# Value and output projections in visits of two token tiles, PSUM places for side work only within a step of its due time

## The chip, the cores and the metric

The kernel runs on one core of one Trainium2 chip. The metric is the device time of one execution in microseconds (us); lower is better. The core has five engines with an instruction queue each: TensorE (PE in the profile, its weight loads PEld), VectorE (DVE), ScalarE (ACT), GpSimd (POOL) and SyncE (SP, which here only issues DMAs). Each engine works through its own queue in order, and engines wait for each other through semaphores.

## What is computed

A block of a diffusion transformer with adaptive layer norm, on x of 2 x 2048 x 256 in fp32: attention with 16 heads, then a gated feed-forward network with 704 hidden units whose inputs and weights are rounded to a 4-bit float in blocks of 16.

```python
h = _layernorm(x, axis=-1) * (1 + ca) + sa
q = einsum('bnd,hkd->bnhk', h, query_proj)      # 16 heads, key size 16
k = einsum('bnd,hkd->bnhk', h, key_proj)
v = einsum('bnd,hvd->bnhv', h, value_proj)      # value size 64
sim = einsum('bnkh,bmhk->bnhm', q, k)
attn = softmax(sim * 0.25, axis=1)              # over the queries n
o = einsum('bnhm,bmhv->bnhv', attn, v)
x = x + ga * einsum('bnhv,dhv->bnd', o, output_proj)
h = _layernorm(x, axis=-1) * (1 + cb) + sb
h = silu(fp4_linear(h, w_gate)) * fp4_linear(h, w_up)
x = x + gb * fp4_linear(h, w_down)
```

The softmax runs over the queries, so one tile of 128 keys m with all 2048 queries is complete in itself.

## The kernel before

**Steps.** The attention is 512 steps: 2 batch entries x 16 heads x 16 tiles of 128 keys. A step computes the scores of one key tile against all 2048 queries in two halves of 1024 (tile `ps`). VectorE takes each half out of PSUM into `e`, scaled and negated, with its minimum. GpSimd combines the two minima (`mn`), ScalarE does the exponential of all 2048 with its sum (`z`), VectorE the reciprocal `rz`, GpSimd scales the 64 values of the key tile by it (`vn`), and TensorE multiplies `vn` with `e` and adds to the head's output `o` (function `step`). `scores` writes the halves.

**Side work.** Everything else is threaded between the steps: projections of q and k (`qk`), of values for four heads at a time (`values`, "quad" q, tile `v`), the output projection of four heads, added to x (`project`, tile `op`), the rounding and transposing of the feed-forward weights, the layer norm of the second batch entry, and the whole feed-forward network of the first. Only the feed-forward network of the second batch entry comes behind the attention, as a tail (`tail`).

**Three uses of the TensorE array.** The scores contract over 64 rows (a stacked q and k), so two matmuls lie side by side in the rows of the array (profile form `64*128`). `o`, `v`, `op` and most of `qk` and the network of the first batch entry write 64 output rows each, two side by side in the columns (`128*64`; function `twin`). Transposes and the tail use the full array (`128*128`). The planner calls these modes "rows", "columns" and "full".

**PSUM.** Two banks hold `o` (pool `ps_o`). The other six are three places of two banks, room `s` (1024 fp32 per partition each). A half of scores takes a whole place. Side work takes a place and also the one token of room `misc` (`OTHER = ["s", "misc"]`), so that at most one side job holds a place at a time; `leave` gives both back.

**The planner.** Each job is a generator that hands out operations (`Op`) and waits (`Wait`). The class `Order` merges them, with estimated durations, into one order for each of TensorE, VectorE, ScalarE and GpSimd when the program is built; the chip sees only that order. A job gets a due time in steps (`add`), becomes active `AHEAD = 5` steps before it, and `settle` lets it pass a `Wait` when its keys are done and its rooms have something free. Among operations that could start within a patience of the earliest, the one with the earliest due goes first (`run`). `order.step` follows the last score group that was emitted.

**Groups of scores.** Two halves at least are emitted together, as one `Group`. When TensorE gets to it, `run` calls `grow`, which adds a third half (limit `GROUP = 3`) if a place is free by then. A group is one visit to the "rows" mode.

**Values and output projection.** `values(b, q, g)` does four token tiles (g runs over four groups of them): 16 matmuls into the whole place, then one copy of 128 x 1024 into `v` by ScalarE or VectorE, whichever the planner finds sooner (`copy`). `project(b, q, g)` likewise does four token tiles, and VectorE adds the 128 x 1024 to x. There are 32 such value visits and 28 such projection visits; the last quad's output projection of the second batch entry is another function, `project_last`. `spread_over` spreads the due times of a quad's visits over a stretch of steps: for values from 13 steps ahead of the quad to 3 into it.

Of the kernel before, what the change touches and what calls it, by code (L numbers as in the profile page):

```python
# [10 lines left out]
F32 = mybir.dt.float32  # L11
# [4 lines left out]
ALU = mybir.AluOpType  # L16
# [4 lines left out]
P = 128  # L21
EPS = 1e-5

MISC = 1
AHEAD = 5
PPE = 0.12
CHANGE = 0.1
PDVE = 0.04
PACT = 0.05
GROUP = 3  # L30
LAG = 4.5
HALF = 0.22
WPACE = 0.5
# [75 lines left out]
class Order:  # L109
# [7 lines left out]
    def __init__(self, rooms, ahead, patience):  # L117
        self.rooms = {name: [(0.0, i) for i in range(n)] for name, n in rooms.items()}
        self.ahead, self.patience = ahead, patience
        self.clock = dict.fromkeys(self.SAME, 0.0)  # L120
        self.done, self.counts = {}, {}
        self.later, self.active = [], []
        self.step, self.seq, self.table, self.chain = 0.0, count(), None, None
        self.port = 0.0
        self.mode = None

    def add(self, gen, due, pace=0.0):

# [27 lines left out]
    def settle(self, c):  # L156

        while isinstance(c.what, Wait):
            w = c.what
            if any(k not in self.done for k in w.after):  # L160
                return False
            if any(len(self.rooms[r]) < w.take.count(r) for r in w.take):
                return False
            times = [self.done[k] for k in w.after]
            taken = [heapq.heappop(self.rooms[r]) for r in w.take]
            times += [t - (w.early if n else 0.0) for n, (t, _) in enumerate(taken)]
            c.base = max([c.base] + [t + self.CROSS for t in times])
            self.advance(c, [place for _, place in taken])
            if c not in self.active:
                return False  # L170
        return True

    def run(self):
        while self.later or self.active:
# [6 lines left out]
            for c in sorted(self.active, key=lambda c: c.due):  # L181
# [25 lines left out]
                for f in found:  # L207
                    best.setdefault(f[4][0].engine, []).append(f)
            if not best:
                if not self.later:  # L210
                    raise RuntimeError(
                        "no chain can go on: "
                        + str([(c.due, vars(c.what)) for c in self.active[:20]])
                    )
                self.step = self.later[0][0] - self.ahead
                continue
            picks = []
            for e, found in best.items():
# [5 lines left out]
                picks.append((start, due, next(self.seq), c, ops))  # L224
            start, _, _, c, ops = min(picks)
            e = ops[0].engine
            t = start
# [98 lines left out]
def adaln_block(  # L326
# [585 lines left out]
    def qk(b, blk, i, n):  # L912

        room = "v" if (b, blk) == (0, 0) and (i == 1 or n % 2) else "st"
        place, _, _ = yield Wait([("ht", b, n), "wk" if i else "wq"], [*OTHER, room])
        if (b, i, blk) not in scratch:
            scratch[b, i, blk] = dram.tile(
                [P, 2, N], F32, tag=f"qk{i}_{blk}", name=f"scr{b}_{i}_{blk}"
            )
        ps = banks(place, f"qk{b}_{blk}_{i}_{n}")[:, 0, :]  # L920
        cols = slice(n * 512, (n + 1) * 512)
        pairs = [
            (wqk_sb[:, i, k, blk * P : (blk + 1) * P], h_t[b][:, k, cols]) for k in range(KC)
        ]
        if (b, blk) == (0, 0):
            for op in matmuls(ps, pairs):
                yield Free(op)
        else:
            ops = twin(ps, pairs)
            for k in range(KC):  # L930
                yield Free(ops[2 * k : 2 * k + 2])
        name = f"st{b}_{blk}_{i}_{n}"
        if room == "v":
            st = vp.tile([P, 4, QV], F32, tag="v", name=name).bitcast(F32R)
            st = st.rearrange("p (r u) n -> p r (u n)", r=2)
        else:
            st = w2.tile([P, 2, 512], F32R, tag="st", name=name, bufs=1)
        yield A.copy(st[:, 0, :], ps)
        yield V.tensor_tensor(st[:, 1, :], ps, st[:, 0, :], ALU.subtract)
        leave(place)  # L940
        st = st.bitcast(F32)
        if (b, blk) == (0, 0):
            if (0, 0) not in heads:
                yield Wait(take=["head"])
                new_head(0, 0)
            q, k = heads[0, 0]
            if i == 0:
                c = n // 2
                yield from stack_q(q, st[0:KD], n % 2, slice(c * 512, (c + 1) * 512))
                signal("first q", of=NCH)  # L950
            else:
                yield from stack_k(k, st[0:KD], cols)
                signal(("first k", n))
        c = n if i == 1 else q_chunk(n)
        yield S.dma_start(scratch[b, i, blk][:, :, c * 512 : (c + 1) * 512], st)
        give(room)
        signal(("qk", b, blk), of=2 * NCH)
        if b == 0 and blk == NB - 1:
            signal("h free", of=2 * NCH + NG)

    def load_head(b, h):
        yield Wait([("qk", b, h // HB)], ["head"])
# [19 lines left out]
        )  # L982
        signal(("wv", b, q))

    def values(b, q, g):
        yield Wait([("ht", b, g), ("wv", b, q)], ["v"])
        v = vs[b, q, g] = vp.tile([P, 4, QV], F32, tag="v", name=f"v{b}_{q}_{g}")
        place, _ = yield Wait(take=OTHER)
        ps = banks(place, f"v{b}_{q}_{g}")
        for j in range(4):  # L990
            m = 4 * g + j
            yield Free(
                twin(
                    ps[:, j // 2, j % 2 * QV : (j % 2 + 1) * QV],
                    [
                        (h_t[b][:, k, m * P : (m + 1) * P], wvs[b, q][:, k, :])
                        for k in range(KC)
                    ],
                )
            )  # L1000
        yield copy(
            v.rearrange("p (i j) n -> p i j n", i=2),
            ps.rearrange("p i (j n) -> p i j n", n=QV),
        )
        leave(place)
        signal(("v", b, q, g))
        if signal(("v", b, q), of=NG):
            give("wv")
        if b == 0 and q == NQUAD - 1:
            signal("h free", of=2 * NCH + NG)  # L1010


    o_acc = {}
# [4 lines left out]
    def scores(i, b, h):  # L1018
# [3 lines left out]
        while n < 2 * NT:  # L1022
# [27 lines left out]
            def grow(t):  # L1050
# [5 lines left out]
                    return False  # L1056
                if n % 2 == 0 and not (order.rooms["e"] and order.rooms["e"][0][0] <= t):
                    return False
                if order.rooms["s"][0][0] > t:
                    return False  # L1060
                half(heapq.heappop(order.rooms["s"])[1])
                return True

            for place in places:
# [9 lines left out]
    def step(i, b, h, m):  # L1074
# [21 lines left out]
        yield A.activation(e, e, AF.Exp, bias=mn[:, 2:3], scale=-1.0, accum_out=z)  # L1096
        rz = small.tile([P, 1], F32, tag="rz", name=f"rz{b}_{h}_{m}")
        yield V.reciprocal(rz, z)
        yield Wait([("v", b, h // 4, m // 4)])
        vn = small.tile([P, VD], F32, tag="vn", name=f"vn{b}_{h}_{m}")  # L1100
        yield G.tensor_scalar(
            vn,
# [58 lines left out]
                G.tensor_tensor(w[:, j, :], w[:, j, :], mod(b, "ga"), ALU.mult)  # L1161
        signal(("wo", b, q))

    def project(b, q, g):

        last = [("out", b, q - 1, 4 * g + j) for j in range(4)] if q else []
        place, _ = yield Wait([("osb", b, q), ("wo", b, q), ("x", b, g)] + last, OTHER)
        ps = banks(place, f"op{b}_{q}_{g}")
        for j in range(4):
            t = 4 * g + j  # L1170
            yield Free(
                twin(
                    ps[:, j // 2, j % 2 * D : (j % 2 + 1) * D],
                    [
                        (o_sb[b, 2 * q + k][:, t * P : (t + 1) * P], wos[b, q][:, k, :])
                        for k in range(2)
                    ],
                )
            )
        if signal(("projected", b, q), of=NG):  # L1180
# [10 lines left out]
        for j in range(4):  # L1191
            signal(("out", b, q, 4 * g + j))

    def project_last(b, q, t, n):

# [307 lines left out]
        add(qk(0, 0, 1, g), -48 if g == 0 else 4 * g - 3.5)  # L1503
    add(load_wv(0, 0), -40)
    for g in range(NG):
        add(values(0, 0, g), -5 if g == 0 else 4 * g - 3)
# [21 lines left out]
    for b in range(B):  # L1528
# [6 lines left out]
        for q in range(NQUAD):  # L1535
            e0 = s0 + 4 * q * NT
            if (b, q) != (0, 0):
                add(load_wv(b, q), e0 - 2 * NT)
                spread_over([values(b, q, g) for g in range(NG)], e0 - NT + 3, e0 + 3)
            add(load_wo(b, q), e0 + 2 * NT)  # L1540
            if (b, q) == (B - 1, NQUAD - 1):
                continue
            o0 = e0 + 4 * NT + 2
            spread_over(
                [project(b, q, g) for g in range(NG)], o0, o0 + (20 if q == NQUAD - 1 else 40)
            )
        if b < B - 1:
            f0 = s0 + PER + 10
# [68 lines left out]
```

## Time and profile before

| what | value |
|---|---|
| median of three runs | 1956.62 us (1956.03 to 1957.0) |
| profiled execution, its own time | 1956.12 us |
| its span, first to last instruction | 1953.7 us |
| TensorE matmul busy | 1910.6 us, 98% |
| VectorE busy | 1704.3 us, 87% |
| ScalarE busy | 1327.6 us, 68% |
| GpSimd busy | 619.8 us, 32% |
| DMA | 88.00 MB, mean 45 GB/s |
| mean granted TensorE clock | 0.999 |

Busy is the time in which at least one instruction of the engine was under way. Matmuls overlap each other, so a group's mean duration times its count is more than its busy time; what counts for TensorE is the distance from the start of one stretch of matmuls to the start of the next. In the timeline, an entry "x8" means eight records merged. A plain fp32 matmul leaves two records, the scores' matmul (a rounded fp32 type) one, so "ps ... x4" is two halves of scores and "o ... x8" the output matmuls of one step. The profile knows nearly all operations under one line, L264, since a helper records them; they are told apart by their tiles.

### The profile page before, as it was taken

Reading aid. Unit: us, or ns where it says so; the run is one execution under the profiler, and the core shown is the slowest. Engines: PE = TensorE matmul, PEld = TensorE weight load, DVE = VectorE, ACT = ScalarE, POOL = GpSimd, SP = SyncE. Lnnn points to the kernel's source line nnn. Section 1 sums busy time; section 2 is a strip of 40 time slices with the busy share of each in tenths; the row PEclk is TensorE's granted clock in tenths of the full one; section 3 lists DMA queues with packets and bytes.
Section 4 is the critical chain, followed back from the end, with each engine's and each line's share of the span. In section 5 each row is a group of like instructions: output and inputs, shape, how many; then the busy total and the mean of one; then the engine's idle time right before and its main releaser. Section 6 shows DMA issues by size and latency. Waiting matters only on the chain. (4 is left out here: it accounts for less than half of the span.)

```text
span 1953.7 us, 30223 instructions
## 1 busy us (share of the span) xinstructions
PE 1910.6 (98%) x10212; PEld 782.6 (40%) x10212; DVE 1704.3 (87%) x4114; ACT 1327.6 (68%) x1427; POOL 619.8 (32%) x1387
## 2 busy tenths in 40 slices
PE   8999999999999999999999999999999999999998
PEld 5323333333333333343334444334433333335666
DVE  5899989999999998889898788888788878997997
ACT  3677767777777677776777567667677877784333
POOL 0233333333334331112444344454353211230010
PEclk9999999999999999999999999999999999999999
DMA  6321121112111122121012201211011111100000
GB/s 205 82 64 53 46 60 49 39 34 50 33 46 33 39 66 81 55 71 46 18 47 60 52 27 45 55 36 26 21 36 44 33 33 33 39 1 1 12 17 17
DMA packets 40393, 88.00 MB, mean 45 GB/s; under 512 B 6320, under 2 KB 22576, under 8 KB 36272
## 3 DMA queue, kind: packets, MB, share of 16 engines
q1 hardware_dynamic: 38880, 83.98, 16.8%
q10 hardware_dynamic: 1360, 2.10, 0.3%
q8 instruction: 82, 1.34, 0.3%
q14 instruction: 71, 0.58, 0.1%
HBM read 63.51 MB, written 20.97 MB: 43 GB/s over the span
## 5 line engine op out<-in xcount | busy, mean ns | idle before, releaser
L264 DVE TENSOR_SCALAR_CACHE_REDUCE e<-ps 128x1024 f32<-128x1024 f32 x1024 | 1225.4, 1216 | 123.9 <-PE ps L264 96.1
L264 ACT ACTIVATE e<-e,mn 128x2048 f32<-128x2048 f32 x512 | 1025.2, 2003 | 417.6 <-POOL mn L264 412.5
L264 PE MATMUL o<-e,vn 128*64 128x512 f32 x4096 | 991.8, 603 | 14.6 <-POOL vn L264 10.4
L264 PEld LDWEIGHTS o<-e,vn 128*64 128x64 f32 x4096 | 252.9, 136 | 479.8 <-issue 380.0
L264 POOL TENSOR_SCALAR mn<-mn 128x1 f32<-128x1 f32 x512 | 153.7, 300 | 751.6 <-DVE rz L264 287.8
L264 PE MATMUL ps<-q,k 64*128 64x512 f32 x2048 | 379.7, 447 | 5.5 <-DVE e L264 2.0
L264 PEld LDWEIGHTS ps<-q,k 64*128 64x128 f32 x2048 | 157.9, 184 | 367.1 <-DVE rz L264 92.0
L264 POOL TENSOR_SCALAR vn<-v,rz 128x64 f32<-128x64 f32 x512 | 167.2, 327 | 348.6 <-DVE rz L264 263.0
L264 PE MATMUL op<-wo,osb 128*64 128x256 f32 (+1 forms) x960 | 122.9, 382 | 3.1 <-DVE x L264 1.8
L264 PE MATMUL v<-wv,ht 128*64 128x256 f32 x1024 | 122.1, 385 | 0.6 <-DVE st L264 0.6
L264 DVE RECIPROCAL rz<-z 128x1 f32<-128x1 f32 x512 | 80.4, 157 | 24.5 <-ACT e L264 23.8
L264 PEld LDWEIGHTS op<-wo,osb 128*64 128x64 f32 (+1 forms) x960 | 73.9, 140 | 57.2 <-issue 18.9
L264 ACT ACTIVATION_READ_ACCUMULATOR e<-e,mn 128x1 f32 x512 | 95.5, 186 | 0.0
L264 PEld LDWEIGHTS v<-wv,ht 128*64 128x64 f32 x1024 | 71.2, 138 | 53.8 <-issue 16.3
L264 DVE DVE_READ_ACCUMULATOR e<-ps 128x1 f32 x1024 | 84.8, 83 | 0.0
L264 ACT COPY osb<-o 64x512 f32<-64x512 f32 x106 | 61.3, 579 | 7.4 <-PE o L264 5.9
L264 PE MATMUL qk<-ht,wqk_sb 128*64 128x512 f32 (+1 forms) x224 | 62.6, 598 | 1.7 <-ACT ht L264 0.9
L264 POOL TENSOR_TENSOR h<-h,m 128x704 f32<-128x704 f32 x32 | 54.2, 1692 | 11.6 <-DVE m L264 3.2
L264 DVE TENSOR_TENSOR x<-op,x 128x1024 f32<-128x1024 f32 (+2 forms) x33 | 37.0, 1122 | 15.6 <-PE op L264 15.3
L264 PE MATMUL dn<-wdb,e 117*128 117x256 f32 (+1 forms) x192 | 45.0, 382 | 3.3 <-ACT e L264 3.1
L264 PE MATMUL dn<-wd_t,h2t 117*64 117x256 f32 (+1 forms) x384 | 46.8, 381 | 0.0
L264 ACT ACT_TABLE_LOAD x34 | 43.6, 1283 | 4.3 <-issue 3.7
(242 smaller groups left out, 1449.8 us busy)
## 6 DMA issues: line engine op xcount, KB each, us to landing
k<-scr SPq DMA_DIRECT2D x124, 256.0 KB, 4.8
scr<-st SPq DMA_DIRECT2D x32, 512.0 KB, 3.1
q<-scr SPq DMA_DIRECT2D x124, 128.0 KB, 5.8
x<-in_x_dram SPq DMA_DIRECT2D x8, 512.0 KB, 4.6
wv<-in_wv_dram SPq DMA_DIRECT2D x8, 256.0 KB, 3.0
wo<-in_wo_dram SPq DMA_DIRECT2D x8, 256.0 KB, 4.0
xt<-in_x_dram SPq DMA_DIRECT2D x4, 512.0 KB, 7.5
out_dram<-h2t SPq DMA_DIRECT2D x16, 128.0 KB, 1.7
```

The lines of the kernel that those rows point to most:

```text
L264: op = Op(self.name, *self.estimate(method, args, kw, lambda: f(*args, **kw)))
```

## The change

`values` and `project` take a parameter `half` and do two token tiles into one bank of the place, with a copy or add of 128 x 512; a quad has eight visits of each in place of four, spread over the same stretch of steps. A value tile `v` is allocated by its first half. A wait in `step` for the values is for the half that holds its key tile.

`settle` holds back a job that wants the `misc` token while it is due more than `PLACE_AHEAD = 1.0` steps ahead of the current step, unless no job at all can go on (`force`).

`grow` takes a place for the third half also when it comes free up to `PATIENCE = 0.1` us later than TensorE would get there; the planner adds that wait to the cost of the first matmul of this half.

```diff
+PLACE_AHEAD = 1.0
+PATIENCE = 0.1
@@ settle
             if any(len(self.rooms[r]) < w.take.count(r) for r in w.take):
                 return False
+            if "misc" in w.take and c.due > self.step + PLACE_AHEAD and not self.force:
+                return False
@@ run
             if not best:
+                if not self.force:
+                    self.force = True
+                    continue
...
+            self.force = False
@@ values
-    def values(b, q, g):
-        yield Wait([("ht", b, g), ("wv", b, q)], ["v"])
-        v = vs[b, q, g] = vp.tile([P, 4, QV], F32, tag="v", name=f"v{b}_{q}_{g}")
+    def values(b, q, g, half):
+        after = [("ht", b, g), ("wv", b, q)]
+        if half == 0:
+            yield Wait(after, ["v"])
+            vs[b, q, g] = vp.tile([P, 4, QV], F32, tag="v", name=f"v{b}_{q}_{g}")
+            signal(("v room", b, q, g))
+        else:
+            yield Wait([*after, ("v room", b, q, g)])
+        v = vs[b, q, g]
         place, _ = yield Wait(take=OTHER)
-        ps = banks(place, f"v{b}_{q}_{g}")
-        for j in range(4):
-            m = 4 * g + j
+        ps = banks(place, f"v{b}_{q}_{g}_{half}")[:, 0, :]
+        for j in range(2):
+            m = 4 * g + 2 * half + j
...
-        yield copy(
-            v.rearrange("p (i j) n -> p i j n", i=2),
-            ps.rearrange("p i (j n) -> p i j n", n=QV),
-        )
+        yield copy(v[:, 2 * half : 2 * half + 2, :], ps.rearrange("p (j n) -> p j n", n=QV))
         leave(place)
@@ grow
-                if order.rooms["s"][0][0] > t:
+                free, place = order.rooms["s"][0]
+                if free > t + PATIENCE:
                     return False
-                half(heapq.heappop(order.rooms["s"])[1])
+                heapq.heappop(order.rooms["s"])
+                first = len(group)
+                half(place)
+                group[first].cost += max(0.0, free - t)
                 return True
@@ step
-        yield Wait([("v", b, h // 4, m // 4)])
+        yield Wait([("v", b, h // 4, m // 4, m % 4 // 2)])
@@ project
-    def project(b, q, g):
+    def project(b, q, g, half):
...
-        for j in range(4):
-            t = 4 * g + j
+        for j in range(2):
...
-        x4 = xs[b, g]
-        yield V.tensor_tensor(
-            x4.rearrange("p (i j) d -> p i j d", i=2),
-            ps.rearrange("p i (j d) -> p i j d", d=D),
-            x4.rearrange("p (i j) d -> p i j d", i=2),
-            ALU.add,
-        )
+        x2 = xs[b, g][:, 2 * half : 2 * half + 2, :]
+        yield V.tensor_tensor(x2, ps.rearrange("p (j d) -> p j d", d=D), x2, ALU.add)
@@ where the jobs are added
-                spread_over([values(b, q, g) for g in range(NG)], e0 - NT + 3, e0 + 3)
+                spread_over(
+                    [values(b, q, g, half) for g in range(NG) for half in range(2)],
+                    e0 - NT + 3,
+                    e0 + 3,
+                )
```

More of the change, by code (lines that the diff above doesn't have):

```diff
@@ L224, in run @@
                 picks.append((start, due, next(self.seq), c, ops))
+            self.force = False
             start, _, _, c, ops = min(picks)
@@ L958, in qk @@
         if b == 0 and blk == NB - 1:
-            signal("h free", of=2 * NCH + NG)
+            signal("h free", of=2 * NCH + 2 * NG)
     def load_head(b, h):
@@ L983, in load_wv @@
         signal(("wv", b, q))
[L985 to L987 removed]
+    def values(b, q, g, half):
[7 more added lines that the diff above has]
+        v = vs[b, q, g]
         place, _ = yield Wait(take=OTHER)
[L989 to L991 removed]
+        ps = banks(place, f"v{b}_{q}_{g}_{half}")[:, 0, :]
+        for j in range(2):
+            m = 4 * g + 2 * half + j
             yield Free(
                 twin(
[L994 removed]
+                    ps[:, j * QV : (j + 1) * QV],
                     [
@@ L1000, in values @@
             )
-        yield copy(
-            v.rearrange("p (i j) n -> p i j n", i=2),
-            ps.rearrange("p i (j n) -> p i j n", n=QV),
-        )
+        yield copy(v[:, 2 * half : 2 * half + 2, :], ps.rearrange("p (j n) -> p j n", n=QV))
         leave(place)
-        signal(("v", b, q, g))
-        if signal(("v", b, q), of=NG):
+        signal(("v", b, q, g, half))
+        if signal(("v", b, q), of=2 * NG):
             give("wv")
         if b == 0 and q == NQUAD - 1:
-            signal("h free", of=2 * NCH + NG)
+            signal("h free", of=2 * NCH + 2 * NG)
     o_acc = {}
@@ L1162, in load_wo @@
         signal(("wo", b, q))
-    def project(b, q, g):
-        last = [("out", b, q - 1, 4 * g + j) for j in range(4)] if q else []
+    def project(b, q, g, half):
+        t = 4 * g + 2 * half
+        last = [("out", b, q - 1, t + j) for j in range(2)] if q else []
         place, _ = yield Wait([("osb", b, q), ("wo", b, q), ("x", b, g)] + last, OTHER)
-        ps = banks(place, f"op{b}_{q}_{g}")
-        for j in range(4):
-            t = 4 * g + j
+        ps = banks(place, f"op{b}_{q}_{t}")[:, 0, :]
+        for j in range(2):
             yield Free(
                 twin(
-                    ps[:, j // 2, j % 2 * D : (j % 2 + 1) * D],
+                    ps[:, j * D : (j + 1) * D],
                     [
-                        (o_sb[b, 2 * q + k][:, t * P : (t + 1) * P], wos[b, q][:, k, :])
+                        (o_sb[b, 2 * q + k][:, (t + j) * P : (t + j + 1) * P], wos[b, q][:, k, :])
                         for k in range(2)
@@ L1179, in project @@
             )
-        if signal(("projected", b, q), of=NG):
+        if signal(("projected", b, q), of=2 * NG):
             give("osb", 2)
             give("wo")
-        x4 = xs[b, g]
-        yield V.tensor_tensor(
-            x4.rearrange("p (i j) d -> p i j d", i=2),
-            ps.rearrange("p i (j d) -> p i j d", d=D),
-            x4.rearrange("p (i j) d -> p i j d", i=2),
-            ALU.add,
-        )
+        x2 = xs[b, g][:, 2 * half : 2 * half + 2, :]
+        yield V.tensor_tensor(x2, ps.rearrange("p (j d) -> p j d", d=D), x2, ALU.add)
         leave(place)
-        for j in range(4):
-            signal(("out", b, q, 4 * g + j))
+        for j in range(2):
+            signal(("out", b, q, t + j))
     def project_last(b, q, t, n):
@@ L1505, in adaln_block @@
     for g in range(NG):
-        add(values(0, 0, g), -5 if g == 0 else 4 * g - 3)
+        for half in range(2):
+            add(values(0, 0, g, half), -5 if g == 0 else 4 * g - 3)
     steps = [(b, h, m) for b in range(B) for h in range(H) for m in range(NT)]
@@ L1544, in adaln_block @@
             spread_over(
-                [project(b, q, g) for g in range(NG)], o0, o0 + (20 if q == NQUAD - 1 else 40)
+                [project(b, q, g, half) for g in range(NG) for half in range(2)], o0, o0 + (20 if q == NQUAD - 1 else 40)
             )
```

## The prediction

> **What bounds the kernel now.** I read the shares of busy time first, then the same by stage, then TensorE's waits, then TensorE's timeline.
>
> ```profile
> PE 1910.6 (98%) x10212; PEld 782.6 (40%) x10212; DVE 1704.3 (87%) x4114; ACT 1327.6 (68%) x1427; POOL 619.8 (32%) x1387
> ```
>
> ```profile
> 105.00:800.00 695.00, 679.60 (x3572) 242.34 (x3570) 648.58 (x1543) 509.39 (x526) 239.74 (x588) 1.00 0.19 48
> 800.00:1780.00 980.00, 973.83 (x5470) 376.88 (x5467) 824.36 (x1874) 707.76 (x737) 351.17 (x743) 1.00 0.15 38
> 1780.00:1954.00 174.00, 158.67 (x675) 115.38 (x674) 154.94 (x472) 56.69 (x96) 13.66 (x11) 1.00 0.04 13
> ```
>
> The second view gives, for each stretch, its length and then the busy time of PE, PEld, DVE, ACT and POOL. TensorE is busy for all but 15 us of 695 and all but 6 of 980: it is the bound of the attention. VectorE is close behind it in the first 800 us (93%) and well behind later (84%). So only what TensorE does or waits for moves the end, and in the first 800 us more work on VectorE could become a wait.
>
> ```profile
> PE o L264 <- POOL vn L264: 10.4, 17, 1.8
> ...
> PE o L264 <- ACT osb L264: 2.5, 3, 1.6
> PE ps L264 <- DVE e L264: 2.0, 5, 0.7
> ```
>
> These are TensorE's waits: total, times, longest. Inside the attention it mostly waits for the scaled values `vn`, the last link of the chain that begins with the scores. Waits for a place that VectorE has to empty (`ps` on `e`) are 2.0 us in the whole run.
>
> ```profile
> 423.54 0.73 PE L264 MATMUL ps<-q,k 64*128 64x512 f32 x4
> 424.21 1.94 PE L264 MATMUL o<-e,vn 128*64 128x512 f32 x8
> 426.07 0.73 PE L264 MATMUL ps<-q,k 64*128 64x512 f32 x4
> 426.74 2.79 PE L264 MATMUL o<-e,vn 128*64 128x512 f32 x12
> 429.36 1.03 PE L264 MATMUL v<-wv,ht 128*64 128x256 f32 x8
> 430.33 0.73 PE L264 MATMUL ps<-q,k 64*128 64x512 f32 x4
> ...
> 436.26 0.97 PE L264 MATMUL ps<-q,k 64*128 64x512 f32 x6
> 437.16 2.79 PE L264 MATMUL o<-e,vn 128*64 128x512 f32 x12
> 439.89 0.73 PE L264 MATMUL ps<-q,k 64*128 64x512 f32 x4
> ```
>
> TensorE's timeline, start and duration. Starts are what to read. A visit to the scores with two halves lasts 426.74 - 426.07 = 0.67 us, one with three 437.16 - 436.26 = 0.90: a half costs 0.23, and 0.67 - 0.46 = 0.20 is the fixed price of the visit. The `o` stretch of 12 records that is followed by `v` (same mode) lasts 429.36 - 426.74 = 2.62 us, the one followed by scores 439.89 - 437.16 = 2.73: leaving the column mode costs 0.11. Without a change of mode eight records are 0.86 to 0.87 (values, half the columns); the `v` stretch between `o` and scores is 0.97 (leaving: +0.10), and another between scores and `o`, from 420.81 to 421.73, is 0.92 (entering: +0.05). So one visit to the scores costs 0.20 + 0.10 + 0.05 = 0.35 us beside its work.
>
> [...] here VectorE alone empties the scores, 1024 times 1216 ns, and is at 93% early. [...] a copy of 1024 out of PSUM takes 1222 ns and one of 512 takes 683 ns, so the split costs 2 x 683 - 1222 = 144 ns.
>
> **The change, part by part.** A planner writes the order, so I counted in the listings of both programs' instructions, engine by engine.
>
> *TensorE, work.* Both have the same 6348 matmuls with the same shapes; halving a visit changes no matmul. Changes of mode fall from 1094 to 1032. Visits to the scores fall from 504 to 471: those with two halves from 456 to 343, those with three from 32 to 107. 33 visits less at 0.35 us are 11.5 us; changes between the column and the full mode rise from 86 to 90, at about 0.1 us each (fitted over the stretches) 0.4 us. Fitted over all 1389 stretches of the trace (a price per matmul by shape, one per kind of change) and summed over each program's listing, TensorE's own work goes from 1893.5 to 1882.7 us. I take **-10.9 us**, in full on the path since TensorE is the bound. The fit leaves 60 us of the span as waits: 43.1 seen as idle, 16.9 inside stretches that begin late.
>
> *The wait in a group.* There are 75 more visits of three halves, and the third may be planned to wait up to 0.1 us for VectorE to hand over its place. Bounds 0 and 75 x 0.1 = 7.5 us; no row of before shows it. Behind it on TensorE's queue are the `o` matmuls, but they would have started only after the same visit. I take the middle, **+3.7**.
>
> *Waits for `vn`.* From a step's first score matmul to its first `o` matmul there lie on average 10.67 us of TensorE work before and 11.87 after, by the listings and the prices above. Steps with less than 7 us are 54 before and 19 after; less than 6 us, 18 and 4. The chain between them is two evictions, minimum, exponential with its sum, reciprocal and scaling: 2 x 1.15 + 0.30 + 2.0 + 0.19 + 0.16 + 0.33 = 5.3 us and the hand-overs. The short ones are those that waited. Bounds: 10.4 us gone, or none. I take half gone, **-5**.
>
> *VectorE.* Value copies there are 10 of 1024 before, 28 of 512 after (ScalarE: 22 of 1024, then 36 of 512); adds to x are 28 of 1024, then 56 of 512. Start to start by the trace's durations, VectorE's work over the whole program goes from 1674 to 1685 us, +11. In the first 224 steps it goes from 661 to 666 while TensorE's goes from 687.5 to 682.6: the margin shrinks from 26 to 17 us, and waits for places should grow. Bounds: none, since TensorE's side is still the larger, or the whole 11 us. I take **+2.5**, a little over a second time the 2.0 us of `ps` on `e`.
>
> *The places.* 64 + 56 visits in place of 32 + 28 hold a place, each from its first matmul to the next user's for 4.1 us (values) and 4.9 us (projections) of TensorE work on average, before 8.0 and 10.4; the sum is 576 before, 554 after. That is why more scores come in threes. The restriction to one step ahead moves side work later. The last value visit of a quad starts 7 to 10 us ahead of its first `o`, before 8 to 15; a copy of 512 takes 0.6, so nothing is late.
>
> *Queues.* Values and projections issue no DMA, but the loads of `wv` and `wo` wait for their ends: on SP's queue they move behind the k and q loads of one head; the values' own loads are asked for 32 steps ahead. The q and k projections' writes move too; the last for the second batch entry is 49 us of TensorE work ahead of its first scores (before 34), and a write and a load land in 3.1 and 4.8 us. On POOL the `wo` scaling moves with its load, 34 steps ahead of the first projection. All free. The last 424 matmuls, the tail, are the same in the same order.
>
> Sum: -10.9 + 3.7 - 5 + 2.5 = **-9.7 us**. The profiled execution took 1956.1 us (span 1953.7 and 2.4 around it), 0.5 below the median of the runs; from the median I get 1956.6 - 9.7 = **1946.9 us**.
>
> **Rivals.** *More of it:* scores run so far ahead that nearly all `vn` waits and part of the hidden 16.9 us go, and the places in threes are free in time: -10.9 - 10 + 2 = -19, 1938 us. For it: the short distances fall to a third. Against: of the 43 us of idle time 3.9 lie ahead of the first scores and 15.3 behind the last step, where the order stays.
>
> *Eaten up:* VectorE's extra 11 us all come onto the path early on: -10.9 + 11 = 0, 1956.6 us. For it: 93% busy in that stage. Against: TensorE's sum stays the larger there.
>
> *Slower:* the short side visits hand their place over quickly. A place left by a side job is taken again with less than 1.8 us of TensorE work between in 103 of 300 cases, before in 57 of 240. A copy of 0.6 us that comes behind a score eviction of 1.15 with hand-overs needs some 2.0 to 2.3, so TensorE could wait 0.5 us at each of the 46 new ones: +23 - 10.9 = +12, 1969 us. It decides when 30 of the 46 wait that long. For it: both engines are nearly full. Against: of the 57 before, almost none shows as a wait (`ps` on `e` 5 times).
>
> *Not what it says:* the listing shows the halved visits and longer groups, so this falls away.
>
> **How the numbers follow.** Forecast 0.63 (1942 to 1952), more of it 0.17, eaten up 0.11, slower 0.09. What a measurement tells from no change here is 0.2%, 3.9 us. Faster is the first two and a little of the third's edge: 0.82; same 0.09; slower 0.09. The range that leaves out two in ten, over the bounds of the unknown terms (-10.9 + 7.5 on one side, nearly -19 on the other): 1939 to 1953.
>
> **What would show it.** Right: `ps` stretches of x6 become about a quarter of the score visits, and the starts still give 0.35 us for a visit; `o` on `vn` falls below 10.4 us; TensorE's busy time falls by about 10 with its share still 98%; the tail lasts as long as before. Wrong: `ps` on `e`, or `op` and `v` on their copies, at several times 2.0 us; VectorE near 97% in the first 800 us with TensorE below; score visits of x6 lasting well over 0.90 us, which would be the wait in the group.

## The result, and the profile after

The changed kernel takes 1929.24 us (median of 4 runs, 1929.0 to 1930.48) against 1956.32 us before (4 runs, 1955.49 to 1957.0): a ratio of 0.9863, 95% interval 0.9846 to 0.988, or 27 us less. Its profiled execution took 1929.38 us, with a span of 1927.6. The forecast was 1946.9 us and a range of 1939 to 1953: the direction was right, the gain nearly three times as large.

The busy times on the page of the changed kernel:

```profile
PE 1898.0 (98%) x10212; PEld 787.2 (41%) x10212; DVE 1711.0 (89%) x4170; ACT 1317.7 (68%) x1428; POOL 617.2 (32%) x1387
```

TensorE's busy time fell by 12.6 us with the same 10212 records; VectorE's rose by 6.7. The span fell by 26.1, so about half of that is not busy time but idle time of TensorE. Its busy times by stage, after the attention's start (the second stretch is shorter by what was gained; columns PE, PEld, DVE, ACT, POOL):

```profile
105.00:800.00 695.00, 687.59 (x3634) 248.96 (x3634) 658.07 (x1575) 511.48 (x534) 238.35 (x590) 1.00 0.19 50
800.00:1755.00 955.00, 952.38 (x5389) 374.67 (x5386) 817.34 (x1882) 687.98 (x719) 347.08 (x733) 1.00 0.15 37
1755.00:1928.00 173.00, 157.57 (x670) 114.41 (x668) 154.08 (x469) 56.70 (x96) 13.66 (x11) 0.99 0.04 13
```

TensorE idles 7.4 us in the first stretch where it idled 15.4, and 2.6 in the second where it idled 6.2. The tail is untouched: 15.4 us of idle time, before 15.3. VectorE is busy 9.5 us more in the same 695 us, in part because more of the kernel is done by then, so it had that time to give.

TensorE's waits in the changed kernel (total, times, longest; lines left out are marked "..."):

```profile
PE o L273 <- ACT osb L273: 2.2, 5, 0.7
PE o L273 <- POOL vn L273: 2.0, 4, 0.6
...
PE ps L273 <- DVE e L273: 1.7, 3, 1.2
```

The wait for `vn` went from 10.4 us in 17 places to 2.0 in 4. The wait for VectorE to empty a place did not grow (1.7 us, before 2.0).

A stretch of its TensorE timeline:

```profile
426.93 0.96 PE L273 MATMUL ps<-q,k 64*128 64x512 f32 x6
427.82 1.94 PE L273 MATMUL o<-e,vn 128*64 128x512 f32 x8
429.59 1.90 PE L273 MATMUL v<-wv,ht 128*64 128x256 f32 x16
431.42 0.49 PE L273 MATMUL ps<-q,k 64*128 64x512 f32 x2
431.84 1.94 PE L273 MATMUL o<-e,vn 128*64 128x512 f32 x8
433.71 0.96 PE L273 MATMUL ps<-q,k 64*128 64x512 f32 x6
434.60 1.94 PE L273 MATMUL o<-e,vn 128*64 128x512 f32 x8
```

Value visits are now x16 (two tiles). Three halves of scores still take 427.82 - 426.93 = 0.89 us from start to start, and `o` x8 before a visit 433.71 - 431.84 = 1.87, as before: these stretches became neither faster nor slower. The visit of one half (x2) takes 431.84 - 431.42 = 0.42, so two further halves cost 0.47, and the fixed price of a visit is again 0.2. Visits of one half are rare, 12 by the listing of before and 17 of the changed kernel, though the groups were described as two halves at least.

**Where the 26 us are.** With the prediction's fitted prices, the work of TensorE is 1893.5 us before and 1882.7 after. The rest of the span is waiting: 60.2 us before, 44.9 after. So 10.9 us came from 62 fewer mode changes and 15.3 from less waiting, where the prediction had 1.2 us more waiting. The level of both sums rests on the fit: a second one over the same stretches, by least absolute deviations, puts each 5.4 us higher and so the waiting lower, with the same difference of 10.9. Taking the waiting apart by the stretch of matmuls that it delays (idle time ahead of it, and time by which a stretch is longer than its price):

| waiting of TensorE, us | before | after | predicted change | measured change |
|---|---|---|---|---|
| idle ahead of `o` (of it for `vn`) | 14.6 (10.4) | 5.9 (2.0) | -5 | -8.7 (-8.4) |
| inside visits of three halves of scores | 1.0 | 5.0 | +3.7 | +4.0 |
| inside visits of two halves of scores | 13.9 | 5.8 | +2.5, for places | -8.1 |
| all else | 30.7 | 28.2 | 0 | -2.5 |

Of the 13.9 us inside visits of two halves before, 2.7 are one visit at 43.37 us, the first scores, which wait for the load of `q` and not for a place. In the changed kernel this wait is gone, so the other visits account for some 5.4 of the 8.1 us.

### The profile page after: what moved, and what is told of

It is laid out like the page before. It is cut to its first block, busy times and chain, and to the rows that moved or that the text cites. A ratio compares the mean times of both kernels' runs of the same rounds, so it can differ in the third digit from the quotient of the medians.

```text
span 1927.6 us, 30282 instructions
## 1 busy us (share of the span) xinstructions
PE 1898.0 (98%) x10212; PEld 787.2 (41%) x10212; DVE 1711.0 (89%) x4170; ACT 1317.7 (68%) x1428; POOL 617.2 (32%) x1387
## 3 DMA queue, kind: packets, MB, share of 16 engines
q1 hardware_dynamic: 38880, 83.98, 16.9%
## 4 chain that ended last, share of the span: by engine, by line
PE 84%; DVE 13%; ACT 2%; issue 1%; POOL 0%; ACTq 0%; POOLq 0%; DVEq 0%
PE o L273 43%; PE ps L273 15%; DVE e L273 8%; PE op L273 6%; PE v L273 6%; PE dn L273 3%; PE qk L273 2%; PE up L273 2%; PE gate L273 2%; PE h2t L273 1%; DVE w L273 1%; PE pg L273 1%; PE pu L273 1%; ACT e L273 1%; PE busy L273 1%
## 5 line engine op out<-in xcount | busy, mean ns | idle before, releaser
L273 DVE TENSOR_SCALAR_CACHE_REDUCE e<-ps 128x1024 f32<-128x1024 f32 x1024 | 1226.1, 1215 | 90.5 <-PE ps L273 65.6
L273 PE MATMUL ps<-q,k 64*128 64x512 f32 x2048 | 371.4, 445 | 2.2 <-DVE e L273 1.7
L273 PEld LDWEIGHTS op<-wo,osb 128*64 128x64 f32 (+1 forms) x960 | 74.3, 140 | 61.1 <-issue 22.6
L273 ACT COPY osb<-o 64x512 f32<-64x512 f32 x104 | 60.2, 579 | 23.6 <-PE o L273 21.7
L273 POOL TENSOR_TENSOR h<-h,m 128x704 f32<-128x704 f32 x32 | 54.1, 1689 | 12.6 <-DVE m L273 7.9
L273 DVE TENSOR_TENSOR x<-op,x 128x512 f32<-128x512 f32 (+1 forms) x61 | 41.2, 676 | 13.7 <-PE op L273 13.3
```

Source lines behind the costliest of these rows:

```text
L273: op = Op(self.name, *self.estimate(method, args, kw, lambda: f(*args, **kw)))
```

## The experiments

In the tables below "work" is the sum of the fitted prices over a program's listing, "waiting" the profiled span less that, "side share" the part of the three places' time that side work keeps, by the banks and the order in the listing: from the end of the last matmul into a place by its earlier user to the end of side work's own last matmul.

### The three parts of the change, alone and in pairs

The first theory (A) took the waits to follow from how far the scores run ahead; the rival (B) took the short visits to free their places sooner. Each kernel is one of the two given ones with a part added or taken out.

Two-tile visits alone:

```diff
-PLACE_AHEAD = 1.0
+PLACE_AHEAD = 100.0
-PATIENCE = 0.1
+PATIENCE = 0.0
```

> The halved visits alone: no step-ahead rule, no wait in a group. By its listing TensorE's work is 1892.3 us (before 1893.5, the changed kernel 1882.7), and 94 steps have less than 7 us of TensorE work from their scores to their output matmuls (before 54, changed 19). Theory A (how far the scores run ahead decides the waits; by the two known runs waits beside the work are about 37 us plus 0.43 us for each such step): 1892 + 77 + 2 = 1971 us, slower than before. Rival B (short visits free their places sooner, and that took the waits away): waits as in the changed kernel, 45 us, 1892 + 45 + 2 = 1939 us.

1959.63 us, ratio 1.0016 (1.0009 to 1.0022): slightly slower. Rival B falls, and A's size is off too, by 11 us.

The step-ahead rule alone, in the kernel before:

```diff
+PLACE_AHEAD = 1.0
...
+            if "misc" in w.take and c.due > self.step + PLACE_AHEAD and not self.force:
+                return False
```

> The step-ahead rule alone, with four-tile visits and no wait in a group. Listing: work 1892.3 us, 15 steps under 7 us. Theory A: 1892 + 43 + 2 = 1938 us. Rival B: the waits of before stay, 60 us: 1892 + 60 + 2 = 1954 us.

1941.54 us, ratio 0.9924 (0.9909 to 0.9939), between A's 1938 and B's 1954 but near A. This one condition brings 15 us. The span falls by 13.9, of which 1.2 are work, 7.4 waits for `vn` and 4.5 waits inside visits of two halves. The waits of TensorE, with the two-tile visits alone:

```profile
PE o L273 <- POOL vn L273: 14.8, 30, 1.6
```

And with the rule alone:

```profile
PE o L272 <- POOL vn L272: 3.0, 5, 1.0
...
PE ps L272 <- DVE e L272: 1.9, 4, 0.7
```

Before, the waits for `vn` were 10.4 us in 17 places. Two-tile visits alone make them worse, the rule alone takes most of them away.

The wait in a group alone, in the kernel before:

```diff
-                if order.rooms["s"][0][0] > t:
+                free, place = order.rooms["s"][0]
+                if free > t + PATIENCE:
```

> The wait of up to 0.1 us in a group alone. Listing: work 1890.5 us, 61 steps under 7 us. Theory A: 1890.5 + 63 + 2 = 1956 us. Rival B: 1890.5 + 60 + 2 + some 1 of waits in the 22 more groups of three = 1954 us. Both say no or little change; were it well below 1950, the wait in the group would be the cause of what was missed.

1957.59 us, ratio 1.0007 (0.9998 to 1.0016): nothing, as both said.

The changed kernel with four-tile visits (`values` and `project` and their due times as before):

> The changed kernel without the halved visits: the step-ahead rule and the wait in a group with four-tile visits. Listing: work 1881.9 us, 16 steps under 7 us. Theory A: as fast as the changed kernel, 1882 + 44 + 2 = 1928 us. Rival B: the waits of before, 60 us: 1944 us.

1937.03 us, ratio 0.9903 (0.9889 to 0.9918). It lies midway between A's 1928 and B's 1944: the rule and the wait in a group bring 20 us without any halved visit, and halving them adds 8 us on top in these two orders.

The two pairs that were left, with two-tile visits and one of the other parts:

```diff
-PLACE_AHEAD = 1.0
+PLACE_AHEAD = 100.0
```

> The changed kernel without the step-ahead rule: halved visits and the wait in a group. Listing: work 1889.7 us; side work keeps 27.8% of the time of the three places (before 25.1%, changed 22.5%). Theory C (side work that takes a place ahead of its time starves the scores of places, and that makes the waits): waits as with the halved visits alone, 65 us, and 3 us for the waits in groups: 1889.7 + 65 + 2 = 1957 us. Rival D (each of the three parts takes some waits away by itself): waits of 50 to 55, 1945 us.

1956.46 us, ratio 1.0001 (0.9992 to 1.0009): without the rule the whole gain is gone, as theory C expected and D did not.

```diff
-PATIENCE = 0.1
+PATIENCE = 0.0
```

> The changed kernel without the wait in a group: halved visits and the step-ahead rule. Listing: work 1889.1 us, 68 groups of three. Theory C: the changed kernel's 45 us of waits less some 3 us of waits in groups: 1889 + 42 + 2 = 1933 us, so the wait in a group is worth about 4 us net. Rival D: waits fall less without it, 50 us, 1941 us.

1931.06 us, ratio 0.9875 (0.9861 to 0.989), near C's 1933 and not D's 1941.

All eight together:

| two-tile visits | rule | wait in group | time, us | work | waiting | side share |
|---|---|---|---|---|---|---|
| no | no | no | 1956.3 | 1893.5 | 60.2 | 25.1% |
| yes | no | no | 1959.6 | 1892.3 | 65.6 | 27.8% |
| no | no | yes | 1957.6 | 1890.5 | 63.3 | 25.2% |
| yes | no | yes | 1956.5 | 1889.7 | 65.0 | 27.8% |
| no | yes | no | 1941.5 | 1892.3 | 47.5 | 20.2% |
| no | yes | yes | 1937.0 | 1881.9 | 53.2 | 20.0% |
| yes | yes | no | 1931.1 | 1889.1 | 40.1 | 22.6% |
| yes | yes | yes | 1929.2 | 1882.7 | 44.9 | 22.5% |

The rule is worth 15, 21, 27 and 29 us in its four pairs of rows. The wait in a group lowers the work by 6 to 10 us with the rule and pays 5 to 6 us of that back as waiting. Two-tile visits do next to nothing without the rule. The side share alone does not order the kernels: with the rule, two-tile visits have the larger share and the shorter time.

What the rule prevents can be seen in the trace of the kernel before. By the listing's banks, a place that held scores until 499.0 us went next to an output projection; the planner gave it the place at step 145, and it was due at 150. Its first matmul came at 512.71. TensorE's timeline there:

```profile
498.29 0.73 PE L264 MATMUL ps<-q,k 64*128 64x512 f32 x4
498.95 1.94 PE L264 MATMUL o<-e,vn 128*64 128x512 f32 x8
500.82 0.73 PE L264 MATMUL ps<-q,k 64*128 64x512 f32 x4
501.48 2.79 PE L264 MATMUL o<-e,vn 128*64 128x512 f32 x12
504.21 0.73 PE L264 MATMUL ps<-q,k 64*128 64x512 f32 x4
504.87 2.79 PE L264 MATMUL o<-e,vn 128*64 128x512 f32 x12
507.60 0.73 PE L264 MATMUL ps<-q,k 64*128 64x512 f32 x4
508.26 2.96 PE L264 MATMUL o<-e,vn 128*64 128x512 f32 x12
511.14 0.73 PE L264 MATMUL ps<-q,k 64*128 64x512 f32 x4
511.81 1.08 PE L264 MATMUL o<-e,vn 128*64 128x512 f32 x4
512.71 1.90 PE L264 MATMUL op<-wo,osb 128*64 128x256 f32 x16
```

For 13.7 us no side matmul runs, yet the scores have two places only, and every visit is one of two halves. There is no idle time in the lines; the cost is the mode changes and a lead that shrinks: the lines hold the scores of five steps and the outputs of six. Gaps over 6 us between a place's last user and side work are 34 in the listing of before (17 of them behind scores, the others behind another side job), 30 with two-tile visits alone, 16 with the rule alone and 9 in the changed kernel.

How often it happens can be counted in the planner as it builds the kernels. After the first step side work takes a place 193 times in the kernel before, 71 of them more than one step ahead of its due time; with two-tile visits alone it is 118 of 253, and with the rule none, in any of its four kernels. That more visits mean more early takes, and that this is why two-tile visits don't help by themselves, fits all eight kernels; only the limit of one step was run, no value between it and none.

### Why two-tile visits help under the rule

Two readings: the shorter operation on VectorE ahead of the scores' evictions (H1), or the shorter hold of the place (H2). The first kernel keeps four-tile visits and splits only their copy or add:

```diff
-        yield copy(
-            v.rearrange("p (i j) n -> p i j n", i=2),
-            ps.rearrange("p i (j n) -> p i j n", n=QV),
-        )
+        for i in range(2):
+            op = copy(v[:, 2 * i : 2 * i + 2, :], ps[:, i, :].rearrange("p (j n) -> p j n", n=QV))
+            yield op
...
+        for i in range(2):
+            x2 = x4[:, 2 * i : 2 * i + 2, :]
+            yield V.tensor_tensor(x2, ps[:, i, :].rearrange("p (j d) -> p j d", d=D), x2, ALU.add)
```

> The step-ahead rule and the wait in a group with four-tile visits, but the visit's copy or add is two of 512 in place of one of 1024. So the place is held as long as with whole visits, and VectorE's queue is never blocked by a side operation for longer than with halved visits. Listing: work 1882.8 us. Theory H1 (a long side eviction on VectorE ahead of the scores' evictions is what the halved visits took away): waits as in the changed kernel, 45 us, 1882.8 + 45 + 2 = 1930 us. Rival H2 (the shorter hold of the place is what counts): waits as with whole visits, 53 us, 1938 us.

1939.5 us, ratio 0.9914 (0.99 to 0.9929): no better than unsplit (1937.0), and far from H1's 1930. This speaks against H1, but it is one order, and orders scatter by as much (below).

Only the output projections halved:

> As the changed kernel, with only the output projections halved and the values in four tiles. Listing: work 1881.4 us. H1: the projections' adds are all on VectorE, most value copies on ScalarE, so nearly the whole gain of the halved visits stays: 45 to 47 us of waits, 1929 us. H2: about half of it: 49 us, 1932 us.

1934.98 us, ratio 0.989 (0.9873 to 0.9906).

Only the values halved:

> As the changed kernel, with only the values halved and the projections in four tiles. Listing: work 1884.6 us. H1: little of the waits goes, 52 us, 1938.5 us. H2: about half, 49 us, 1935.5 us.

1937.21 us, ratio 0.9902 (0.9887 to 0.9917). Against the 1937.0 us with neither, the projections bring 2 us and the values nothing, together less than the 8 us of both, so H2's sums (1932 and 1935.5) don't fit closely either; the scatter below is of the same size. H2 is not shown.

### How much one order is worth

A due time shifted by 0.1 steps means nothing by itself but gives a different order. The values' in the changed kernel:

```diff
-                    e0 - NT + 3,
+                    e0 - NT + 3.1,
```

> The changed kernel with the values' due times 0.1 steps later, which means nothing by itself but gives another order. Listing: work 1884.1 us, 36 steps under 7 us (changed kernel: 1882.7 and 19). If the planner's order is fragile: 5 to 8 us slower than the changed kernel, 1936 us. If not: within 2 us of it, 1930 us. It gives the size of a difference between two kernels that may be put down to a part of the change.

1939.28 us, ratio 0.9915 (0.99 to 0.9929): 10 us slower than the changed kernel.

```diff
-            o0 = e0 + 4 * NT + 2
+            o0 = e0 + 4 * NT + 2.1
```

> The kernel before with the output projections' due times 0.1 steps later. Listing: work 1893.8 us, 36 steps under 7 us (before 1893.5 and 54). Fragile: several us faster, 1949 us. Not fragile: within 2 us of before.

1954.39 us, ratio 0.9992 (0.9984 to 1.0001): no difference clear of noise. Two more shifts, of the output projections (2) and of the second block of q and k projections (4), each with two-tile visits (halved) and with four-tile visits (whole):

> The changed kernel with the output projections' due times 0.1 steps later. Listing: work 1882.8 us (changed kernel 1882.7). If the changed kernel's 1929 us is a lucky order among halved ones and 1939 us an unlucky one: 1934 us. If 1929 us is what halved visits give and the first nudge was the exception: 1929 us.

1936.94 us, ratio 0.9901 (0.9885 to 0.9918).

> The changed kernel with the due times of the second block of q and k projections 0.1 steps later. Listing: work 1883.1 us. Lucky order: 1934 us. Rule of halved visits: 1929 us.

1930.28 us, ratio 0.9866 (0.9851 to 0.9881).

> Four-tile visits with the step-ahead rule and the wait in a group, the output projections' due times 0.1 steps later. Listing: work 1883.7 us (without the nudge 1881.9, 1937 us on the chip). If halved visits are worth 5 us or more by themselves: 1938 to 1941 us, above all halved ones but the first nudge. If the difference was luck: as often below 1935 as above.

1942.21 us, ratio 0.9929 (0.9914 to 0.9943).

> Four-tile visits as above, with the second block of q and k projections 0.1 steps later. Listing: work 1882.3 us. Halved visits worth 5 us or more: 1936 to 1940 us. Luck: 1930 to 1936 us.

1939.97 us, ratio 0.9916 (0.9901 to 0.9931).

Under the rule, with the wait in a group, four orders with two-tile visits take 1929.2, 1930.3, 1936.9 and 1939.3 us and three with four-tile visits 1937.0, 1940.0 and 1942.2. In the three pairs with the same due times, the two-tile form is faster by 7.8, 5.3 and 9.7 us. So it has a worth of its own of some 5 to 10 us, and the given kernel is the fastest of four orders whose mean is 1933.9. The traces say where it lies: in these pairs the waits inside visits of two and three halves fall by 7.7, 3.1 and 8.2 us, and the idle time ahead of `o` by 1.2, 5.7 and 2.3. Time by stage, from the traces, cut by the count of score matmuls:

| stage | before | changed | shifted values | halved 2 | halved 4 | whole | whole 2 | whole 4 |
|---|---|---|---|---|---|---|---|---|
| steps 0 to 63, us | 202.9 | 193.8 | 192.4 | 193.8 | 194.0 | 197.7 | 197.7 | 200.0 |
| steps 192 to 255, us | 219.7 | 216.1 | 228.9 | 219.9 | 216.1 | 215.4 | 215.5 | 215.3 |

In the three pairs the two-tile visits gain 4 to 6 us in the first 64 steps; there the first value tiles are made while the first steps run. A part of it is one wait. The first scores with four-tile visits (the kernel `no_halves`):

```profile
43.04 1.11 PE L273 MATMUL ps<-q,k 64*128 64x512 f32 x3
46.06 0.46 PE L273 MATMUL ps<-q,k 64*128 64x512 f32 x1 [1.90 <-DMA q<-st]
```

And in the changed kernel:

```profile
42.38 0.77 PE L273 MATMUL ps<-q,k 64*128 64x512 f32 x4
```

The last loads of `q` ahead of these scores are issued at 42.90 us in the first and at 39.51 in the second, where only two value tiles come ahead of the q projections that they need. All nine traces with four-tile value visits have this wait of 1.9 us, none of the eleven with two-tile value visits has it, and the first `o` matmul comes at 53.5 to 56.2 us in the former and at 50.8 to 52.1 in the latter.

The unlucky order loses 13 us against the changed kernel in steps 192 to 255. VectorE is full in a part of that stage, here in the changed kernel:

```profile
640.00:660.00 20.00, 20.00 (x114) 7.76 (x112) 20.00 (x62) 13.63 (x14) 5.96 (x15) 1.00 0.00 1
660.00:680.00 20.00, 18.96 (x96) 6.46 (x92) 20.00 (x65) 14.12 (x17) 5.48 (x14) 1.00 0.13 35
680.00:700.00 20.00, 17.82 (x92) 5.97 (x92) 19.62 (x52) 15.06 (x17) 9.15 (x18) 1.00 0.42 98
700.00:720.00 20.00, 20.00 (x113) 7.74 (x113) 19.79 (x63) 14.46 (x17) 4.14 (x13) 1.00 0.09 27
```

VectorE (the third pair) works 79.4 of these 80 us, with the second batch entry's layer norm among its work, and TensorE is idle for 3.2. That a lead of the scores lost there comes back only slowly would fit, but was not tested. The order with shifted values, 35 us later:

```profile
754.42 1.08 PE L273 MATMUL o<-e,vn 128*64 128x512 f32 x4
...
756.45 0.16 DVE L273 RECIPROCAL rz<-z 128x1 f32<-128x1 f32 x1
...
756.95 0.32 POOL L273 TENSOR_SCALAR vn<-v,rz 128x64 f32<-128x64 f32 x1
...
757.32 0.65 PE L273 MATMUL o<-e,vn 128*64 128x512 f32 x2 [1.83 <-POOL vn L273]
```

TensorE has run through what it had and waits 1.83 us until the reciprocal and then `vn` of the next step are there.

### The price of a visit, and a longer wait in a group

The changed kernel with two halves per visit at most:

```diff
-GROUP = 3
+GROUP = 2
```

> The changed kernel with score groups of two halves at most. 515 score visits in place of 471, work by the listing 1897.6 us in place of 1882.7; only 4 steps under 7 us of TensorE work. If a score visit costs 0.35 us that no wait hides: 1897.6 + 45 - 5 (the wait in the threes) + 2 = 1940 us. If the price of a visit is mostly covered by waits that come anyway: 1925 to 1930 us.

1948.39 us, ratio 0.996 (0.9945 to 0.9975). By the listing's prices the work is 14.9 us more than in the changed kernel, and the time 19 us more, so the price of 44 more visits is not covered by waits that come anyway, though both expected sums (1940, and 1925 to 1930) were too low. The waiting did not fall but rose to 50.5 us, although by the listing the scores run further ahead than anywhere else. So theory A's measure, how much TensorE work lies between a step's scores and its output, does not by itself predict the waits. The largest waits ahead of `o`:

```profile
PE o L273 <- POOL vn L273: 5.6, 5, 2.0
...
PE o L273 <- DVE osb L273: 3.9, 6, 1.3
PE o L273 <- ACT osb L273: 3.8, 6, 1.1
```

More than half of these are for the copies that empty `o` at the end of a head, which that measure doesn't contain.

The changed kernel with a longer wait in a group, in two orders (the second with the projections' due times 0.2 steps earlier and the feed-forward network's 0.2 later):

```diff
-PATIENCE = 0.1
+PATIENCE = 0.2
```

> The changed kernel with a wait of up to 0.2 us in a group in place of 0.1. Listing: work 1879.5 us (changed 1882.7), 123 groups of three (107). If the waits in groups grow by less than the 3 us of work that they save: 1926 to 1929 us. If they eat it up: 1929 to 1935 us, and what the wait in a group gives is used up at 0.1.

1933.64 us, ratio 0.9882 (0.9867 to 0.9896).

> The same with the output projections' due times 0.2 steps earlier and the feed-forward network's 0.2 later. Listing: work 1881.3 us. As a second order with the longer wait: 1926 to 1930 us if the longer wait pays, 1931 to 1938 us, like the changed kernel with shifted due times, if it does not.

1932.73 us, ratio 0.9877 (0.986 to 0.9893). Inside visits of three halves 9.2 and 8.6 us are waited, in the changed kernel 5.0, while the work is 3.2 and 1.4 us less: the longer wait costs more than it saves there. The times themselves lie inside the scatter of the four orders above. No version tried is faster than the changed kernel.

## Why the prediction was right in direction and wrong in size

- **TensorE's own work, -10.9 us: right.** Prices fitted anew over the changed kernel's own trace give 10.7 us and 0.34 for a visit, and in the kernel with groups of two a visit of two halves lasts the same 0.66 us as before.
- **The wait in a group, +3.7: right**, +4.0 measured inside visits of three.
- **Waits for `vn`, -5: right direction, too small by 3.4 us.** I took half of the bound of 10.4; 8.4 went. The short distances go with these waits in most kernels (94 steps under 7 us and 14.8 us with two-tile visits alone, 54 and 10.4 before, 19 and 2.0 after, 15 and 3.0 with the rule alone), but not in the kernel with groups of two (4 and 5.6), so distance alone is not the mechanism. The distances counted are also not the ones described: 10.67 and 11.87 us match a count from a step's last score matmul; from its first it is 11.8 and 13.5.
- **VectorE, +2.5: the step that failed, with its sign.** It reads "the margin shrinks from 26 to 17 us, and waits for places should grow". VectorE's busy share from 105 to 800 us did rise, from 93% to 95%, and yet TensorE waited 8.1 us less inside visits of two halves (5.4 without the first scores' wait for `q`) and no more for `ps` on `e`. The waits for places were not a matter of VectorE's total time: the rule alone, with VectorE's work nearly as before (1705.5 us busy, before 1704.3), took the waits inside these visits from 13.9 to 9.4 us and those for `vn` from 10.4 to 3.0. From 60 us on, behind the first scores, they are 9.4 to 11.2 us in the five kernels without the rule and 4.4 to 7.7 in the fifteen with it. How a single half comes to wait, presumably for a place that another half has only just left while the third lies with side work, is argued and not shown: in the kernel before, the visits for which side work has or next gets the third place wait 0.027 us each, the others 0.021.
- **The price of a split, 144 ns: about right.** In the changed kernel a copy of 512 takes 688 ns, so 154. Both figures are for VectorE's copies out of PSUM (one of 1024 took 1222 ns in the kernel before).
- **The places: wrong reason.** I put the longer groups down to the shorter hold of halved visits, which I summed from the first matmul of side work on. The time in which a place lies empty ahead of that first matmul was not in this sum, and it is the larger part: by the listings 720 us of before, against 548 us in which side work fills its place. Without the rule the halved visits enlarge it to 856 us, and the kernel gains nothing. The rule alone takes it to some 575 us and the filled time to 446; but in the changed kernel it is some 690 again, over more visits, with 439 filled. So not the sum of empty time decides. What is gone in every kernel with the rule are the places taken more than a step early. The sums given, 576 and 554 us, contain the visits of `project_last`, which the counts beside them leave out.
- **Nothing late, queues and tail free: right.** The tail's idle time is 15.4 us, before 15.3.
- **The rivals.** "More of it" came, beyond its 1938 us: it had the waits for `vn` going and named part of the hidden 16.9 us, but its sum gave nothing for those inside the visits, and it could not know that the order at hand would be a lucky one by some 5 us against the mean of four. "Eaten up" and "slower" rested on VectorE and on quick hand-overs; neither shows, with `ps` on `e` at 1.7 us.
- **The range** was too narrow on the fast side because the two terms of waiting were bounded by the idle time that the waits view names. The 16.9 us hidden inside stretches were counted but not given to any term of the sum.

Still open is the exact share of the two-tile visits: three pairs give 5 to 10 us, in which the early steps' 4 to 6 are steady and the rest scatters. The rule also moves side work later in the order; it was not tried to move it without the early takes, nor to take places early at a fixed rate with everything else equal.

## What to carry to other kernels

A buffer that low-priority work took ahead of its time cost the critical work here even where no wait showed, and the rule against it was worth 15 to 29 us: look at the time between a buffer's take and its first use, and let side work take it only when it is due. TensorE paid 0.35 us for each visit to the row mode. Where an engine pays for a change of mode, count the changes in the program's order; that part of the prediction held to a microsecond here. Where a planner makes the order, try a meaningless shift or two before a few microseconds are put down to a part of a change: here one such shift was worth 10 us. And look at the first operations apart: here some 3 us of a gain that was sought in the whole order were one load at the start.

## What the runs showed of the hardware

- In the kernel before, a visit to the row mode between column-mode matmuls cost 0.35 us beside its matmuls: 0.20 in its own stretch and 0.15 in the stretches around it. A visit of two halves lasted 0.66 us at the median with `o`, `v` or `op` on either side, and in the kernels with 471, 504 and 515 visits.
- A wait of a matmul inside a run of matmuls can be no idle time in the profile: score visits of two halves last 0.66 us at the median before, and nine of them last 0.71 to 0.89 with busy records that follow each other without a gap (0.89 at 1651.51 us). Of the 60 us of waiting before, 17 were of this kind by the first fit and 12 by the second; only distances between starts show them.
